# Holding back the loads of a fused adapter kernel until the first gathered rows have landed, and reordering block 0's sums

## The chip, the cores and the metric

The kernel runs on one core of a Trainium2 chip. A time is the device time of one execution in microseconds (us). A core has five engines that run their own instruction streams and meet at semaphores: PE (TensorE, matrix products into PSUM), DVE (VectorE), ACT (ScalarE), POOL (GpSimd) and SP (SyncE, which here issues the plain DMAs). Gathers by index are issued by POOL. Both kinds of DMA are carried out by the same 16 DMA engines, through a queue of SP's (q1 in the profile) and one of POOL's (q0).

## The reference, cut to what matters

x has 64 sequences of 64 tokens with 1024 features, all in fp32. Two adapter layers are added, one after the other:

```python
B_req = B[adapter_ids]                                    # layer 0: one adapter of rank 16 for each sequence
A_req = A[adapter_ids]
x = x + einsum('bnr,bor->bno', einsum('bni,bri->bnr', x, B_req), A_req)

base   = einsum('btd,od->bto', x, W)                      # layer 1: a dense product ...
logits = einsum('btd,ed->bte', x, Wr) + 5.0 * one_hot(language_ids)
topw, topi = top_k(logits, 2)                             # ... and the best 2 of 8 experts of rank 16
gates  = sum(one_hot(topi) * softmax(topw)[..., None], axis=-2)
h      = einsum('btd,erd->bter', x, A)
x = x + base + 2.0 * einsum('bter,bte,eor->bto', h, gates, B)
```

Below, x1 is x after layer 0. The input x is handed over feature-major (xT), W with its input features on the partitions.

## The kernel before, in words

The 4096 tokens are eight blocks of 512 (eight sequences each). Two blocks make a group of tokens (s = 0 to 3), and for each group the 1024 x 1024 product x1 (W + I) is computed by Strassen's scheme with seven products, on two levels; only the first two products of group 0 ("whole" ones, tile pw) stay on one level. The quarter-size weights made on the way in group 0 (tiles s, m) are stored to DRAM (s_kept) and loaded again in the later groups.

What is done for block k:
- `load` brings x in two halves of 512 features, 1 MB each, tiles ("x", k, 0) and ("x", k, 1). SP issues them.
- `gather` brings 128 rows of 4 KB of each adapter table: gb (B) and ga (A), 512 KB each. POOL issues them by the indices idx, which DVE computes from ids0.
- `turn` transposes gb on PE (tile pt, 4 transposes in each of two steps); ACT copies the result out (bt).
- `project` multiplies x by it on PE, 32 matmuls in four column strips (tile pb). A matmul in fp32 is two instructions in the trace, so pb counts x64 for a block. DVE multiplies by a mask (bx).
- `adapt` multiplies bx by ga for each half of the features (tile px, x32 in the trace for a half), and four DVE steps for each half add the result to x in place, a step for each strip of 128 tokens ("gi"). After that the tile holds x1.
- `rows` multiplies x1 by the routers and the experts' A (a1_sb, which holds the loaded a1 and, in its last 8 columns, wr), tile ph, a step of 16 matmul instructions for each strip j of 128 tokens. `gates` is a row of small DVE steps (top 2 and softmax), and `weigh` transposes the gated h (tile pg).
- `early(k)` is turn, project and adapt; `late(k)` is rows, gates and weigh.

The constants: wr_c and ids1 (32 KB each; ids1 is the language id of each sequence, written to all partitions), a1 (512 KB), b1 (512 KB). `languages` computes the router's bias on DVE from ids1, `spread` copies wr into a1_sb on POOL. `add_identity` adds the identity to the four diagonal quarters w_00, w_11, w_22, w_33 of W on DVE, so that the product gives x1 + x1 W.

**The order is made by a planner** (class Plan). Every step is added with its engine and a cost there, the keys that it reads and writes, a due time `at` and the buffers that it takes. `order` runs a list schedule with fixed costs: it picks the engine that can start a step first, and there, among the steps that can start within 0.2 us of that, the one with the smallest due time. A transfer moves 350 KB per us (`KB`), lands 2.2 us later (`LAND`), a gather lands 4.0 + 2.2 us after its issue (`GATHER`). The steps are then issued in the order of their planned starts, and each engine keeps that program order on the chip: a step whose operands are late holds all that stands behind it on its engine. The semaphores themselves come from the tiles that an instruction really touches, not from the planner's keys; a key that names no common tile orders the plan alone.

Buffers: a buffer of a tag is free for the next tile when the last step that reads or writes a key of the old tile is done. Among them are 4 for "l" (PSUM; pt, pb, px, ph and pg take them), 2 for gb, 2 for ga, one each for bt and bx, 7 for "q" (halves of x and their sums).

Due times of the steps around the change, in planner's units: x of block 0 -58, gb of block 0 -59, wr_c and ids1 -53, a1 -45, the w quarters -43 to -36, x of block 1 -42, its gathers -43 and -42, b1 -29; turn -40 for block 0 and -12 for block 1; project -38 and -10; adapt -37 and -36 for block 0, -9 and -8 for block 1; the sums of block 0 -39 and -38; rows of block 0 -14 to -11; add_identity -30; the first product 0.

In the diff: `Plan.add` and `Plan.order` are the planner, `consts` (L308 on) plans the constants, `load` L353, `gather` L367, `project` L400, `adapt` L428, `load_w` L597, `add_identity` L606, and the calls that set due times stand at L988 to L996. The profile puts nearly all instructions on one line (L29, a helper that issues them), so groups are told apart by their tiles.

Of the kernel before, what the change touches and what calls it, by code (L numbers as in the profile page):

```python
# [14 lines left out]
P = 128  # L15
# [18 lines left out]
class Plan:  # L34
# [22 lines left out]
    def add(self, eng, fn, reads=(), writes=(), at=0.0, take=(), kb=0, sb=False):  # L57

        self.steps.append(
            dict(n=len(self.steps), eng=eng, fn=fn, reads=list(reads), writes=list(writes),  # L60
                 at=at, take=list(take), kb=kb, sb=sb)
        )

    def order(self):
        steps = self.steps
        wrote, read, users, tag_of, turns = {}, {}, {}, {}, {}
        for st in steps:
# [16 lines left out]
            st["dep"] = dep  # L84
        held = [[] for _ in steps]
# [6 lines left out]
        for st in steps:  # L92
            for d in st["dep"]:
                after[d].append(st["n"])
        needs = [len(st["dep"]) for st in steps]
        ready = {st["n"] for st in steps if not st["dep"]}
# [9 lines left out]
        def start(n, e):  # L106
            st = steps[n]
            t = clock.get(e, 0.0)
            if st["kb"] and e == "SP":
                t = max(t, moved - self.AHEAD)  # L110
            for d in st["dep"]:
# [66 lines left out]
def kernel(  # L178
# [129 lines left out]
    def consts():  # L308
# [4 lines left out]
        )  # L313
        plan.add({"SP": 0.4}, lambda e: sp.dma_start(a1_sb[:, :, :P], a1), [], [("a1",)], -45, kb=512)
        plan.add({"SP": 0.4}, lambda e: sp.dma_start(b1_sb, b1), [], [("b1",)], -29, kb=512)
# [23 lines left out]
        plan.add({"DVE": 1.0}, languages, [("ids1",)], [("bias",)], -45)  # L339
# [13 lines left out]
    def load(k, i, at):  # L353
        t = ("x", k, i)

        def fn(e):
            made[t] = new("q", [P, HC, TB], f"x_{k}_{i}")
# [7 lines left out]
        plan.add({"SP": 0.5}, fn, [], part(t), at, [("q", t)], kb=1024)  # L365

    def gather(k, tag, table, at):  # L367
# [9 lines left out]
        plan.add({"POOL": 1.1}, fn, [], [((tag, k),)], at, [(tag, (tag, k))], kb=512)  # L377
# [22 lines left out]
    def project(k, at):  # L400
# [3 lines left out]
        def fn(e):  # L404
            made[pb] = new("l", [P, GT], f"pb_{k}")
            made[bx] = new("bx", [P, GT], f"bx_{k}")
            for c in range(NC):
# [11 lines left out]
        def out(e):  # L419
            dve.tensor_tensor(made[bx], made[pb], mask, ALU.mult)  # L420

        plan.add(
            {"PE": 2.2}, fn, [(("bt", k), 1), (("bt", k), 2)] + whole(k), [(pb,), (bx,)], at,
            [("l", pb), ("bx", bx)],
        )
        plan.add({"DVE": 0.3}, out, [(pb,)], [(bx,)], at - 8)

    def adapt(k, h, at):  # L428
# [33 lines left out]
        for gi in range(NG):  # L462
            xs = part(x, gs=[gi])
            plan.add({"DVE": 0.7}, out(gi), [(px[gi],)] + xs, xs, at - 2)
# [132 lines left out]
    def load_w(i, j, at):  # L597
# [6 lines left out]
        plan.add({"SP": 0.4}, fn, [], [(t,)], at, [("s", t)], kb=256)  # L604

    def add_identity(i, at):  # L606
# [8 lines left out]
        plan.add({"DVE": 0.5}, fn, [(t,), (("bx", 0),)], [(t,)], at, sb=True)  # L615
# [372 lines left out]
    consts()  # L988
    for k, at in ((0, -58), (1, -42)):
        for i in range(2):  # L990
            load(k, i, at)
        gather(k, "gb", b0, at - 1)
# [80 lines left out]
```

## Time and profile before

| | |
|---|---|
| runs of the kernel | 528.85, 531.17, 528.12, 528.79 us; median 528.82 |
| the profiled execution | 528.58 us, its span 526.8 us |
| granted PE clock | 0.999 over the span |
| PE busy | 506.6 us (96%) in 3400 matmul instructions |
| DVE busy | 289.9 us (55%) |
| POOL busy | 183.0 us (35%) |
| ACT busy | 41.2 us (8%) |
| DMA | 99.19 MB, mean 188 GB/s over the span; q1 (SP) 90.26 MB, q0 (POOL) 8.39 MB |

The span runs from the first to the last instruction; the time of an execution also has what lies around it. "Busy" of PE counts pipelined matmuls whose ends are modelled, so 96% is not 96% of its peak. The chain that ended last is PE for 94% of the span, DMA for 3%.

The instructions of the opening that the change is about (start and length in us, from the timeline; PE counts are instructions):

| start | length | what |
|---|---|---|
| 1.19 | 0.97 | SP issues x of block 0, both halves |
| 2.21, 2.75, 3.53 | 0.51, 0.74, 0.65 | SP issues wr_c, ids1, a1 |
| 2.88, 4.30 | 1.11, 0.94 | POOL issues gb and ga of block 0 |
| 4.23 | 10.48 | SP issues the first 4 quarters of w |
| 5.54, 6.79 | 0.94, 0.94 | POOL issues gb and ga of block 1 |
| 10.56 | 1.94 | PE pt x8, after 10.56 idle that the landing of gb ended |
| 12.42 | 2.62 | PE pb x64 of block 0 |
| 14.75 | 2.23 | SP issues x of block 1, both halves |
| 14.98 | 0.66 | PE pt x4 of block 1 (the other 4 at 24.77) |
| 15.46 | 1.14 | DVE lang and bias, after 12.58 idle that ids1 ended |
| 16.52 | 0.28 | DVE bx of block 0 |
| 17.03 | 17.62 | SP issues the other 12 quarters of w |
| 18.60 | 0.49 | DVE adds the identity to w_00, after 1.79 idle that w ended |
| 19.01 | 4.87 | DVE sums of block 0, x8 |
| 25.65 | 0.94 | POOL issues gb of block 3, after pt of block 1 |
| 37.93, 39.41 | 1.00, 0.50 | DVE adds the identity to w_22 and w_33; 4.52 and 0.48 idle before them, until w landed |

### The profile page before, as it was taken

The numbers are of one execution on the slowest core, as the hardware profiler recorded it, in microseconds if no ns is written. First come the engines' busy times: TensorE is split into PE (matmuls) and PEld (weight loads), VectorE is DVE, ScalarE is ACT, GpSimd is POOL, SyncE is SP. The second block draws the span as 40 slices with busy tenths as digits, with TensorE's granted clock in tenths as the row PEclk, the third lists the DMA queues.
The fourth block names the chain that finished last, engine by engine and source line by source line (L and its number), as shares of the span: only waits on it lengthen the run. The fifth ranks groups of instructions, "written<-read, shape, count | busy, mean of one in ns | idle before, by whom it ended". The sixth has DMA issues, their size and how long they took to land.

```text
span 526.8 us, 8463 instructions
## 1 busy us (share of the span) xinstructions
PE 506.6 (96%) x3400; PEld 433.2 (82%) x3400; DVE 289.9 (55%) x554; ACT 41.2 (8%) x81; POOL 183.0 (35%) x149
## 2 busy tenths in 40 slices
PE   1799999999999999999999999999999999999995
PEld 1755768798888988898888998889888898888884
DVE  0639999948964174616674355345567417432632
ACT  1111010002000100011000100000200010001000
POOL 3131955762343234222333313312422323433200
PEclk9999999999999999999999999999999999999999
DMA  8999735768666239736556526744545633610222
GB/s 284 362 364 401 277 136 188 272 225 310 215 197 212 82 111 326 255 110 185 176 191 201 189 82 209 268 161 120 162 163 197 205 95 102 218 41 1 80 81 80
DMA packets 53687, 99.19 MB, mean 188 GB/s; under 512 B 4880, under 2 KB 10000, under 8 KB 53648
## 3 DMA queue, kind: packets, MB, share of 16 engines
q1 hardware_dynamic: 51344, 90.26, 50.3%
q0 software_dynamic: 2304, 8.39, 4.3%
q8 instruction: 27, 0.44, 0.3%
q14 instruction: 12, 0.10, 0.0%
HBM read 69.01 MB, written 29.62 MB: 187 GB/s over the span
## 4 chain that ended last, share of the span: by engine, by line
PE 94%; DMA 3%; DVE 1%; issue 1%; SPq 0%; ACT 0%; DVEq 0%
PE pa L29 37%; PE pb L29 35%; PE ph L29 11%; PE pw L29 6%; PE px L29 3%; DMA ids_sb<-in_ids 2%; PE pt L29 1%; DMA out_T<-o 1%; PE pg L29 1%; DVE o L29 1%; SPq L29 0%; DVE bias L29 0%; ACT o L29 0%; DVE lang L29 0%; DVE bx L29 0%
## 5 line engine op out<-in xcount | busy, mean ns | idle before, releaser
L29 PE MATMUL pa<-ti,s 128*128 128x256 f32 x416 | 99.0, 381 | 0.7 <-ACT o L29 0.7
L29 PE MATMUL pb<-ti,s 128*128 128x256 f32 x376 | 93.4, 380 | 0.0
L29 PEld LDWEIGHTS pa<-ti,s 128*128 128x128 f32 x416 | 77.6, 190 | 12.3 <-ACT o L29 1.1
L29 PEld LDWEIGHTS pb<-ti,s 128*128 128x128 f32 x376 | 70.7, 190 | 9.5
L29 POOL TENSOR_TENSOR ti<-x,ti 128x512 f32<-128x512 f32 x28 | 37.2, 1328 | 85.3 <-PE pb L29 84.2
L29 PEld LDWEIGHTS ph<-a_sb,x 128*128 128x128 f32 x512 | 62.7, 190 | 3.8 <-issue 2.7
L29 PE MATMUL ph<-a_sb,x 128*128 128x136 f32 x512 | 63.3, 279 | 2.1 <-issue 2.1
L29 POOL TENSOR_TENSOR ti<-t,ti 128x512 f32<-128x512 f32 x24 | 33.5, 1396 | 87.3 <-PE pb L29 64.8
L29 POOL TENSOR_TENSOR ti<-x 128x512 f32<-128x512 f32 x26 | 34.2, 1314 | 53.2 <-PE pb L29 31.6
L29 DVE TENSOR_TENSOR o<-pb,o 128x512 f32<-128x512 f32 x45 | 31.1, 690 | 34.1 <-PE pb L29 20.6
L29 PE MATMUL pa<-x,s 128*128 128x256 f32 x208 | 49.8, 379 | 0.0
L29 DVE TENSOR_TENSOR x<-px,x 128x512 f32<-128x512 f32 x64 | 39.8, 683 | 10.4 <-PE px L29 6.1
L29 POOL TENSOR_TENSOR ti<-t 128x512 f32<-128x512 f32 x22 | 29.4, 1339 | 44.1 <-PE pb L29 34.4
L29 PEld LDWEIGHTS pa<-x,s 128*128 128x128 f32 x208 | 38.7, 190 | 4.8
L29 PE MATMUL pa<-t,s 128*128 128x256 f32 x168 | 41.2, 381 | 0.8 <-DVE o L29 0.8
L29 PEld LDWEIGHTS pa<-t,s 128*128 128x128 f32 x168 | 31.4, 190 | 5.7 <-DVE o L29 1.2
L29 DVE TENSOR_TENSOR o<-pa,u 128x512 f32<-128x512 f32 x28 | 19.3, 691 | 26.8 <-PE pa L29 26.2
L29 PE MATMUL pw<-x,w 128*128 128x512 f32 x64 | 28.7, 595 | 0.0
L29 DVE TENSOR_TENSOR u<-pb,u 128x512 f32<-128x512 f32 x21 | 14.5, 689 | 25.5 <-ACT u L29 20.7
L29 DVE TENSOR_TENSOR o<-pa,v 128x512 f32<-128x512 f32 x16 | 11.0, 690 | 27.5 <-PE pa L29 24.6
L29 PE MATMUL pb<-hg,b_sb 128*128 128x256 f32 x88 | 26.2, 379 | 0.0
L29 PE MATMUL pb<-x,s 128*128 128x256 f32 x96 | 23.9, 381 | 0.0
(112 smaller groups left out, 577.3 us busy)
## 6 DMA issues: line engine op xcount, KB each, us to landing
s<-s_kept SPq DMA_DIRECT2D x147, 256.0 KB, 2.7
x<-in_xT SPq DMA_DIRECT2D x16, 1024.0 KB, 5.7
out_T<-o SPq DMA_DIRECT2D x32, 512.0 KB, 3.2
s_kept<-s SPq DMA_DIRECT2D x28, 256.0 KB, 4.2
s_kept<-w SPq DMA_DIRECT2D x18, 256.0 KB, 4.8
w<-in_w SPq DMA_DIRECT2D x16, 256.0 KB, 10.1
s_kept<-m SPq DMA_DIRECT2D x3, 256.0 KB, 5.1
a_sb<-in_a SPq DMA_DIRECT2D x1, 512.0 KB, 14.3
```

What stands on the lines that cost most here:

```text
L29: return self._tc.keep_in_program_order(f(*args, **kwargs))
```

## The change

It has these parts:
- The planner learns `behind`: a step that is planned to start after another has started, with no wait on the chip.
- The second x half of block 0 is made by a POOL memset of one column that stands behind the gather of gb of block 0; SP's load of that half waits for the memset. The gather of ga of block 0 stands behind the memset too.
- a1 waits for a POOL copy of one column of the landed gb of block 0 into a1_sb. b1, the w quarters, x of block 1 and every gather of a later block stand behind a1 (`behind`).
- The order of the loads in the program: x half 0, gb, x half 1, ga of block 0, then wr_c, ids1, a1, b1.
- `project` is two steps, one for each half of the features, each needing only its half of x.
- The sums of block 0 get due times that go strip by strip. `languages` and `add_identity` read x of block 0 (the planner's keys): the one is planned after its loads, the other after its sums. `add_identity` no longer reads ("bx", 0).

```diff
--- before.py
+++ after.py
@@ -54,11 +54,12 @@
         self.slots, self.shared = slots, shared
         self.steps = []
 
-    def add(self, eng, fn, reads=(), writes=(), at=0.0, take=(), kb=0, sb=False):
+    def add(self, eng, fn, reads=(), writes=(), at=0.0, take=(), kb=0, sb=False, behind=()):
+
 
         self.steps.append(
             dict(n=len(self.steps), eng=eng, fn=fn, reads=list(reads), writes=list(writes),
-                 at=at, take=list(take), kb=kb, sb=sb)
+                 at=at, take=list(take), kb=kb, sb=sb, behind=list(behind))
         )
 
     def order(self):
@@ -82,6 +83,7 @@
                 users.setdefault(k[0], set()).add(n)
             dep.discard(n)
             st["dep"] = dep
+            st["begun"] = {d for k in st["behind"] for d in wrote.get(k, ())} - dep
         held = [[] for _ in steps]
         left, last = {}, {}
         for tile_ in tag_of:
@@ -90,10 +92,10 @@
                 held[n].append(tile_)
         after = [[] for _ in steps]
         for st in steps:
-            for d in st["dep"]:
+            for d in st["dep"] | st["begun"]:
                 after[d].append(st["n"])
-        needs = [len(st["dep"]) for st in steps]
-        ready = {st["n"] for st in steps if not st["dep"]}
+        needs = [len(st["dep"] | st["begun"]) for st in steps]
+        ready = {st["n"] for st in steps if not needs[st["n"]]}
         free = {tag: [0.0] * c for tag, c in self.slots.items()}
         turn = {tag: 0 for tag in turns}
         clock, end, where, now = dict(self.SET), {}, {}, {}
@@ -108,6 +110,8 @@
             t = clock.get(e, 0.0)
             if st["kb"] and e == "SP":
                 t = max(t, moved - self.AHEAD)
+            for d in st["begun"]:
+                t = max(t, steps[d]["start"] + 0.1)
             for d in st["dep"]:
                 t = max(t, end[d] + (0.0 if where[d] == e and not steps[d]["kb"] else self.LAG))
             want = {}
@@ -311,8 +315,14 @@
             {"SP": 0.4}, lambda e: sp.dma_start(ids1_sb, ids1[0:1, :].to_broadcast([P, NB])),
             [], [("ids1",)], -53, kb=32,
         )
+
+        def hold(e):
+
+            pool.tensor_copy(a1_sb[:, 0, :1], made["gb", 0][:, :1])
+
+        plan.add({"POOL": 0.2}, hold, [(("gb", 0),)], [("a1",)], -56)
         plan.add({"SP": 0.4}, lambda e: sp.dma_start(a1_sb[:, :, :P], a1), [], [("a1",)], -45, kb=512)
-        plan.add({"SP": 0.4}, lambda e: sp.dma_start(b1_sb, b1), [], [("b1",)], -29, kb=512)
+        plan.add({"SP": 0.4}, lambda e: sp.dma_start(b1_sb, b1), [], [("b1",)], -29, kb=512, behind=[("a1",)])
 
         def spread(e):
             pool.tensor_copy(a1_sb[:, :, P:], wr_c)
@@ -336,7 +346,7 @@
             dve.tensor_scalar(bias, bias, LANG_BIAS, None, ALU.mult)
 
         plan.add({"POOL": 0.3}, spread, [("wr_c",)], [("wr",)], -45)
-        plan.add({"DVE": 1.0}, languages, [("ids1",)], [("bias",)], -45)
+        plan.add({"DVE": 1.0}, languages, [("ids1",)] + whole(0), [("bias",)], -45)
 
 
     made = {}
@@ -353,8 +363,16 @@
     def load(k, i, at):
         t = ("x", k, i)
 
+        held = (k, i) == (0, 1)
+
+        def hold(e):
+
+            made[t] = new("q", [P, HC, TB], f"x_{k}_{i}")
+            pool.memset(made[t][:, 0, :1], 0.0)
+
         def fn(e):
-            made[t] = new("q", [P, HC, TB], f"x_{k}_{i}")
+            if not held:
+                made[t] = new("q", [P, HC, TB], f"x_{k}_{i}")
             sp.dma_start(
                 made[t],
                 xT[i * HC * P : (i + 1) * HC * P, k * TB : (k + 1) * TB].rearrange(
@@ -362,7 +380,12 @@
                 ),
             )
 
-        plan.add({"SP": 0.5}, fn, [], part(t), at, [("q", t)], kb=1024)
+        if held:
+            plan.add({"POOL": 0.1}, hold, [], part(t) + [("gathered",)], at, [("q", t)])
+        plan.add(
+            {"SP": 0.5}, fn, [], part(t), at, [("q", t)] * (not held), kb=1024,
+            behind=[("a1",)] * (k == 1),
+        )
 
     def gather(k, tag, table, at):
         def fn(e):
@@ -374,7 +397,10 @@
                 in_offset=bass.IndirectOffsetOnAxis(ap=idx[:, k : k + 1], axis=0),
             )
 
-        plan.add({"POOL": 1.1}, fn, [], [((tag, k),)], at, [(tag, (tag, k))], kb=512)
+        plan.add(
+            {"POOL": 1.1}, fn, [("gathered",)] * ((tag, k) == ("ga", 0)), [((tag, k),)], at,
+            [(tag, (tag, k))], kb=512, behind=[("a1",)] * (k > 0),
+        )
 
     def turn(k, g, at):
 
@@ -401,10 +427,11 @@
 
         pb, bx = ("pb", k), ("bx", k)
 
-        def fn(e):
-            made[pb] = new("l", [P, GT], f"pb_{k}")
-            made[bx] = new("bx", [P, GT], f"bx_{k}")
-            for c in range(NC):
+        def fn(cs):
+            if cs[0] == 0:
+                made[pb] = new("l", [P, GT], f"pb_{k}")
+                made[bx] = new("bx", [P, GT], f"bx_{k}")
+            for c in cs:
                 for gi in range(NG):
                     strip = slice(gi * CG, (gi + 1) * CG)
                     pe.matmul(
@@ -419,10 +446,13 @@
         def out(e):
             dve.tensor_tensor(made[bx], made[pb], mask, ALU.mult)
 
-        plan.add(
-            {"PE": 2.2}, fn, [(("bt", k), 1), (("bt", k), 2)] + whole(k), [(pb,), (bx,)], at,
-            [("l", pb), ("bx", bx)],
-        )
+
+        for h in range(2):
+            plan.add(
+                {"PE": 1.1}, lambda e, h=h: fn(range(h * HC, (h + 1) * HC)),
+                [(("bt", k), 1), (("bt", k), 2)] + part(("x", k, h)), [(pb,)] + [(bx,)] * (1 - h),
+                at + 0.1 * h, [("l", pb), ("bx", bx)] * (1 - h),
+            )
         plan.add({"DVE": 0.3}, out, [(pb,)], [(bx,)], at - 8)
 
     def adapt(k, h, at):
@@ -461,7 +491,7 @@
         )
         for gi in range(NG):
             xs = part(x, gs=[gi])
-            plan.add({"DVE": 0.7}, out(gi), [(px[gi],)] + xs, xs, at - 2)
+            plan.add({"DVE": 0.7}, out(gi), [(px[gi],)] + xs, xs, at - 2 + 1.5 * gi * (k == 0))
 
     def rows(k, at):
 
@@ -601,7 +631,7 @@
             made[t] = new("s", [P, QC, QO], f"w_{i}{j}")
             sp.dma_start(made[t], w[:, j * QC : (j + 1) * QC, i * QO : (i + 1) * QO])
 
-        plan.add({"SP": 0.4}, fn, [], [(t,)], at, [("s", t)], kb=256)
+        plan.add({"SP": 0.4}, fn, [], [(t,)], at, [("s", t)], kb=256, behind=[("a1",)])
 
     def add_identity(i, at):
 
@@ -612,7 +642,7 @@
                 d = made[t][:, c, c * P : (c + 1) * P]
                 dve.tensor_tensor(d, d, ident, ALU.add)
 
-        plan.add({"DVE": 0.5}, fn, [(t,), (("bx", 0),)], [(t,)], at, sb=True)
+        plan.add({"DVE": 0.5}, fn, [(t,)] + whole(0), [(t,)], at, sb=True)
 
     quarter = {
         (i, j): {(k, l): w_name[2 * i + k, 2 * j + l] for k in range(2) for l in range(2)}
@@ -985,12 +1015,13 @@
         for k in rest:
             step(*k)
 
-    consts()
-    for k, at in ((0, -58), (1, -42)):
-        for i in range(2):
-            load(k, i, at)
+    for k, at in ((0, -60), (1, -42)):
+        load(k, 0, at)
         gather(k, "gb", b0, at - 1)
+        load(k, 1, at)
         gather(k, "ga", a0, at)
+        if k == 0:
+            consts()
     for q0, at in (((0, 0), -43), ((0, 2), -39), ((2, 0), -37), ((2, 2), -36)):
         for i, j in ((0, 0), (1, 0), (1, 1), (0, 1)):
             load_w(q0[0] + i, q0[1] + j, at)
```

## Prediction

> **What bounds the kernel now.** I read the table by stretches first, then the chain that ended last, then the DMA issues of the opening, then single waits.
>
> The table by stretches (length, then busy time and instruction count of PE, PE's weight load, DVE, ACT, POOL; then clock, DMA share, GB/s):
>
> ```profile
> 0.00:10.50 10.50, 0.00 (x0) 0.00 (x0) 1.03 (x7) 1.28 (x1) 4.99 (x14) 1.00 0.78 276
> 10.50:16.80 6.30, 5.08 (x76) 4.25 (x76) 1.26 (x5) 1.76 (x3) 1.21 (x2) 1.00 0.91 314
> 16.80:21.00 4.20, 2.08 (x65) 1.92 (x65) 2.40 (x7) 0.00 (x0) 0.94 (x1) 1.00 1.09 370
> 21.00:29.00 8.00, 8.00 (x69) 8.00 (x70) 5.91 (x11) 0.97 (x2) 0.94 (x1) 1.00 1.04 381
> 29.00:39.40 10.40, 10.40 (x29) 4.38 (x31) 4.36 (x22) 1.77 (x4) 4.97 (x4) 1.00 1.08 362
> 39.40:72.50 33.10, 33.10 (x245) 20.34 (x246) 31.28 (x53) 2.74 (x6) 17.19 (x12) 1.00 0.77 294
> ...
> 130.00:515.00 385.00, 384.95 (x2435) 340.09 (x2435) 194.05 (x371) 26.63 (x53) 118.73 (x90) 1.00 0.48 159
> ```
>
> From 21 us on PE is full: 384.95 of 385 us. Only the opening has idle PE that an early change can win: 10.5 + 1.2 + 2.1 = 13.8 us before 21. And in 39.4 to 72.5 DVE is nearly full too (31.28 of 33.1): PE work pulled forward may only meet DVE there.
>
> The chain that ended last, in order of time (start, length, what):
>
> ```profile
> 2.75 12.68 DMA ids_sb<-in_ids
> ...
> 16.86 2.07 PE px L29 x64
> 18.93 2.06 issue
> 20.99 3.95 PE ph L29 x32
> 24.94 0.44 PE pt L29 x4
> 25.37 3.71 PE ph L29 x32
> 29.08 10.30 PE pw L29 x24
> 39.38 1.89 PE pb L29 x64
> ```
>
> The opening hangs on the language ids, which land at 15.43; then px, DVE's sums, ph, and from 29.08 the products pw. Block 1's projection pb runs at 39.38, behind three products.
>
> The DMA issues of the opening, each from a short stretch around it, us to landing last; the second ga is the gather issued at 65.02, when the queues were quiet:
>
> ```profile
> gb<-in_b,idx POOLq DMA_INDIRECT x1, 7.5
> ...
> x<-in_xT SPq DMA_DIRECT2D x1, 1024.0 KB, 12.4
> ...
> x<-in_xT SPq DMA_DIRECT2D x1, 1024.0 KB, 13.7
> ...
> ga<-in_a,idx POOLq DMA_INDIRECT x1, 4.2
> ```
>
> So gb of block 0 (issued 2.88) lands at 10.4, block 1's first half (issued 14.75) at 27.1 and its second half (16.2) at **29.9**. DMA moves 360 to 410 GB/s from 4 us to 45 with one dip, 234 in 12 to 14.5.
>
> **The change, step by step.** Times are those of the profiled execution (528.58 us, span 526.80, so 1.78 around the span; the median of the runs is 528.82, 0.24 more).
>
> 1. First gather. gb0 keeps its place (2.88). Bounds from issue to landing: 4.2 quiet, 7.5 loaded. x half 0 still flows (1 MB from about 3 to 6 us by the rates) and half 1 comes behind; nearer the loaded row: 6.9, landing 9.8 against 10.4. Gain 0.6 (0 to 3.3).
>
> 2. x half 1 of block 0 goes behind a memset that POOL issues after the gather (which ended at 3.99; POOL's next instruction began 0.3 later): SP issues it at 4.5 instead of 1.66, behind wr_c and ids1. Block 0 is 2 x 1.05 + 2 x 0.52 = 3.15 MB; 0.28 had moved by 4 us, the rest at 0.4 MB/us ends at 11.2. The small loads now run in front of it; they are what ran in the dip (2.5 us at 234 instead of 400: 0.42 MB, 1 us). With about 0.6 to land: 12.8, between 11.4 (as before: 1.66 + 9.8) and 14.
>
> 3. pb's second half is half of 1.95 to 2.62, so about 1.1: it ends at 13.9. Languages (1.14 on DVE) stand ahead of bx, but ids1 now lands behind one x half instead of two and a gap of 13 us; with bx 0.28, **px starts at 14.25** instead of 16.86. The memset, the copy that holds a1 and its semaphore cost POOL 0.1 to 0.3 each while it has nothing else: hidden. SP queues a1, twelve more loads and all of x1 behind that copy; a1 then starts near 10.2 instead of 3.53 and needs until about 14 to 15; ph wants it at 17. Hidden, with 2 us of cover.
>
> 4. Sums. The first identity add waited for w (DMA, 1.79 idle) and held the sums from about 18 to 19.01. It goes behind them: 1.0 gained. By strips, ph could start three sums (0.61 each) after px's first half: 14.25 + 1.1 + 1.8 = 17.2.
>
> 5. But block 1's gathers are now behind the copy. gb1 is issued near 10.2; loaded, 7.8 (gb of 13.59): it lands at 18.0. By the planner's figures (landing 6.2 after issue) block 1's two transposes pt fit between px and ph, and PE's order is fixed by them. So ph waits: 18.0 + 0.66 + 0.60 = 19.3. Four strips at 1.86 (7.44): **ph ends at 26.8** instead of 29.08. So far 2.3 won.
>
> 6. What comes next on PE. add_identity read ("bx", 0) before, so the planner's only bx buffer stayed taken until the last identity add; that, not data, put pb of block 1 at 39.3. Now it reads x of block 0 and the buffer is free after px. Worked with the planner's own constants: a1 starts at 11.7, then w x4, gb1, ga1, x1 half 0 (lands 24.5), gb2, half 1 (lands 28.9); ph ends at 29.1. Both halves of pb (due -10) are then ready at their turn and go **ahead of the first pw** (due 0). On the chip PE reaches that point at 26.8 and must wait for x1's second half.
>
> 7. When does that half land? Ahead of it on SP's queue stand the same bytes as before. On POOL's queue there is one gather more: gb3 is issued when pt frees its buffer, at 19.3 instead of 25.65, so 0.52 MB / 0.39 = 1.3 us move ahead of it. The dip at 12 to 14.5 goes (1.1 less) and the loss of step 2 comes (1.0 more). 29.9 + 1.3 - 1.1 + 1.0 = **31.1**. Bounds: 28.7 (no extra gather, no loss), 33 (a further 2 us with an empty queue while a1's copy waits). Then half of pb, 0.95: the products start at 32.05. Before, the same work (ph, then pb's 1.95) was worth 29.08 + 1.89 = 30.97. Net **+1.1**.
>
> 8. Behind that: the same instructions, PE full. Block 1's sums (8 x 0.61) now fall into DVE's gap before 37.9, where it waited 4.52 us for w; so DVE is about 5 us freer in 39.4 to 72.5. b1 stays last on SP (issued 34.92, landed 6.4 later; its readers start at 46.4, so 5 us of cover). The only bubble the change could remove is 0.68 us at 105. I count nothing for it. Cost if wrong: pg of block 1 began 0.15 us after DVE gave up h (71.59 + 0.69, PE at 72.43), so without the relief each us that w lands later is paid.
>
> Sum: -0.6, -2.0 (px), -1.0, given back in step 5 and by the wait of step 6; 528.82 + 1.1 = **529.9**.
>
> The Trainium skill, page "DMA: Bandwidth & Descriptors", section "Queues, rings and completion order", says that each DMA engine goes round between the queues packet by packet; by that, holding SP's loads back gives a gather little, since it would not have stood behind them. Its section "Anatomy of one DMA — SWDGE (gpsimd) path" gives 2.0 us plus bytes over 436 GB/s, for 512 KB an estimate of 3.2 us; the trace has 7.5 and 4.2. With the page's figure gb0 would land at 6.1 and the transposes start 3.7 us sooner; step 7 and so the sum would stay where they are.
>
> **Rivals.**
> Faster: pb of block 1 stays behind products, or x1 lands by 28. Then step 5's 2.3 is kept, 526.5, and up to 3.9 if gb1 lands near 16 (5.8 after issue): 524.9. For it: DVE is freed. Against it: due -10 against 0, and x1's halves landed at 27.1 and 29.9 with 0.5 MB less beside them.
> Slower: block 1's x is starved. Where both queues are busy POOL's moves more (0.29 MB against 0.10 in 19 to 20 us); with gb1 to gb3 and ga1, ga2 all ahead of it, and an empty queue for 2 us at the start, the second half lands at 34: 34 + 0.95 - 30.97 = +4.0, **532.8**. It passes 0.5% when the half lands after 32.6. For it: five gathers now start within 10 us. Against: the bytes are the same.
> No effect: transfers set everything and x1 lands at 29.9 as before: 528.8.
>
> **How the numbers follow.** Forecast 0.55 (its own range 527.5 to 532), slower rival 0.22, faster 0.17, no effect 0.06. A measurement tells 0.5%, 2.6 us, from no change: 526.2 and 531.5 are the borders. Of the faster case three quarters lie below 526.2, 0.13, and 0.01 of the forecast; of the slower case 0.19 lies above 531.5, and 0.08 of the forecast; same is the rest, 0.59. Low 526.3 and high 532.9 leave about 0.1 on each side.
>
> **What would show it.** Right: PE's order pt, pb, px, pt, ph x64, then pb x64 ahead of the first pw, with an idle PE of 2 to 6 us ended by x in that pb; x half 1 of block 1 landing at 30 to 32; px at 13.5 to 15; gb1's wait ahead of ph. Wrong: pw directly behind ph (then 525 to 526); ph waiting for a1; DVE held by ids1; a wait in 40 to 130 on DVE's products or on w.

## The result, and the profile after

The changed kernel takes 529.51 us (median of 52 executions, 528.75 to 532.61) where the kernel before takes 528.94 us beside it (78 executions, 527.79 to 531.34). The ratio is 1.0019, with a 95% interval of 1.0010 to 1.0027: a loss of 0.5 to 1.4 us, which is real and small. The forecast was 529.9 and the border of "no change" 0.5%. The profiled execution took 529.45 us with a span of 527.7, against 528.58 and 526.8.

The 52 executions lie in two groups with nothing between 529.52 and 530.15: 27 around 529.02 and 25 around 531.03. Those of the kernel before do so too, less clearly: 40 around 528.38 and 38 around 529.91. The profile of after is from the lower group; one from the upper group is shown with the last experiment, and explains it. The median of 529.51 is the upper edge of the lower group; with one execution less there it would lie in the gap.

First the table by stretches of after (length, then busy time and instruction count of PE, PE's weight load, DVE, ACT and POOL; then clock, DMA share, GB/s):

```profile
0.00:10.50 10.50, 0.72 (x4) 0.75 (x5) 2.10 (x11) 1.28 (x1) 4.13 (x16) 1.00 0.71 243
10.50:16.80 6.30, 5.89 (x106) 4.77 (x108) 0.29 (x1) 1.17 (x2) 2.38 (x3) 1.00 1.06 366
16.80:21.00 4.20, 3.95 (x60) 3.51 (x54) 4.10 (x7) 1.08 (x2) 1.87 (x2) 1.00 1.05 379
21.00:29.00 8.00, 6.30 (x71) 6.13 (x73) 3.25 (x12) 0.77 (x2) 4.99 (x4) 1.00 1.04 392
29.00:39.40 10.40, 8.78 (x101) 4.79 (x91) 7.49 (x18) 0.80 (x2) 5.04 (x4) 1.00 1.09 356
39.40:72.50 33.10, 33.10 (x160) 19.47 (x159) 28.73 (x57) 3.82 (x8) 11.84 (x9) 1.00 0.59 220
...
130.00:515.00 385.00, 385.00 (x2430) 340.27 (x2423) 192.85 (x370) 26.63 (x53) 118.52 (x90) 1.00 0.49 160
```

Before 21 us PE is busy 3.4 us more than before (0.72 + 5.89 + 3.95 against 5.08 + 2.08). In the next two stretches, where it was full, it now stands still for 1.70 + 1.62 = 3.3 us. The gain of the opening moved into a new hole, and behind 40 us nothing is left to see.

The timeline of PE shows the hole (start and length in us, out<-in and shapes, count; in brackets the idle time before and what ended it):

```profile
9.78 1.94 PE L29 MATMUL pt<-ident,gb 128*128 128x128 f32 x8 [9.78 <-DMA gb<-in_b,idx]
11.65 3.64 PE L29 MATMUL pb<-x,bt 128*32 128x128 f32 x64
15.71 2.07 PE L29 MATMUL px<-bx,ga 32*128 32x128 f32 x64 [0.41 <-DVE bx L29]
17.71 1.19 PE L29 MATMUL pt<-ident,gb 128*128 128x128 f32 x8
19.15 7.65 PE L29 MATMUL ph<-a_sb,x 128*128 128x136 f32 x64 [0.25 <-issue]
28.50 1.08 PE L29 MATMUL pb<-x,bt 128*32 128x128 f32 x32 [1.70 <-DMA x<-in_xT]
31.19 1.08 PE L29 MATMUL pb<-x,bt 128*32 128x128 f32 x32 [1.62 <-DMA x<-in_xT]
32.20 3.70 PE L29 MATMUL pw<-x,w 128*128 128x512 f32 x8
```

Block 1's pb now runs directly behind ph, ahead of the first product pw, and waits for each half of its x. The chain that ended last goes through that load (start, length, what):

```profile
2.88 6.77 DMA gb<-in_b,idx
13.63 17.52 DMA x<-in_xT
```

It lands at 31.15. Added up from PE's records of the whole span: ph of block 0 ends at 29.08 before and 26.80 after; behind it PE is idle for 1.51 and 4.13 us, and works for 491.36 and 491.90. So PE ends at 521.95 and 522.83: 2.28 won, 2.62 given back as waits, 0.54 as work that takes longer, which I did not trace further. I use these three numbers for each experiment below.

### The profile page after: what moved, and what is told of

Same layout as the page of the kernel before. It is cut to its first block, busy times and chain, and to the rows that moved or that the text cites. A ratio compares the mean times of both kernels' runs of the same rounds, so it can differ in the third digit from the quotient of the medians.

```text
span 527.7 us, 8467 instructions
## 1 busy us (share of the span) xinstructions
PE 508.3 (96%) x3400; PEld 433.9 (82%) x3400; DVE 288.8 (55%) x552; ACT 40.8 (8%) x81; POOL 186.2 (35%) x153
## 4 chain that ended last, share of the span: by engine, by line
PE 93%; DMA 5%; SPq 1%; DVE 0%; issue 0%; POOL 0%
PE pa L29 37%; PE pb L29 36%; PE ph L29 10%; PE pw L29 6%; DMA x<-in_xT 3%; PE px L29 3%; DMA gb<-in_b,idx 1%; PE pt L29 1%; PE pg L29 1%; SPq L29 1%; DMA ids_sb<-in_ids 0%; DVE o L29 0%; DVE idx L29 0%; POOL a_sb L29 0%
## 5 line engine op out<-in xcount | busy, mean ns | idle before, releaser
L29 POOL TENSOR_TENSOR ti<-x,ti 128x512 f32<-128x512 f32 x27 | 35.6, 1318 | 79.4 <-PE pb L29 77.5
L29 POOL TENSOR_TENSOR ti<-t,ti 128x512 f32<-128x512 f32 x23 | 32.0, 1393 | 72.4 <-PE pb L29 55.2
L29 POOL TENSOR_TENSOR ti<-t 128x512 f32<-128x512 f32 x24 | 33.4, 1393 | 49.4 <-PE pb L29 34.5
L29 DVE TENSOR_TENSOR o<-pb,o 128x512 f32<-128x512 f32 x45 | 31.1, 690 | 35.7 <-PE pb L29 21.8
L29 DVE TENSOR_TENSOR u<-pb,u 128x512 f32<-128x512 f32 x21 | 14.5, 689 | 25.6 <-ACT u L29 20.7
```

Source lines behind the costliest of these rows:

```text
L29: return self._tc.keep_in_program_order(f(*args, **kwargs))
```

## The experiments

A median stands beside the median of the kernel before on the same chip (528.7, 529.5 and 528.8 in the three groups of runs). The ratio beside it has its 95% interval in brackets. A profile shows one execution: those of the key alone, the order alone and the loads alone are the longest of their runs, that of the gathers held back the second longest.

### The place of block 1's pb

**Later by 11 units of due time**, all else as in after:

```diff
-        project(k, at + 2)
+        project(k, at + 2 + 11 * (k == 1))
```

> The changed kernel with the projection of block 1 (pb) due after the first product, so that PE runs ph, pw, pb, pw. Theory (the wait for x of block 1 in pb, 3.3 us, is what gave the gain of the opening back): pw starts when ph ends, at 26.8 instead of 32.2; pb comes at 30.4, waits under 1 us for the second half of x (landing near 31.2) and the work ph + pb + pw is done at 32.2 to 33 instead of 35.8: 526 to 527, PE full afterwards. Rival (DVE or the landing of w sets 40 to 72, so an earlier PE only waits there): 528.5 to 529.5, with PE idle of 2 to 3 us between 33 and 75 ended by DVE.

527.97 us, ratio 0.9982 (0.9966 to 0.9999). PE in its timeline:

```profile
19.13 7.65 PE L29 MATMUL ph<-a_sb,x 128*128 128x136 f32 x64 [0.25 <-issue]
26.61 3.60 PE L29 MATMUL pw<-x,w 128*128 128x512 f32 x8
30.14 2.16 PE L29 MATMUL pb<-x,bt 128*32 128x128 f32 x64
```

With one product between ph and pb both waits for x are gone at once, and the kernel beats after. So the hole in after comes from pb's place. But only 1.4 of the 3.3 us show in the span (526.3 against 527.7), and the time lies between what the theory (526 to 527) and the rival (528.5 to 529.5) had. The waits of this kernel (engine, waiting group, what it waited for: total, times, longest) name two new ones, for another pb's x at 91 us and for a DVE step at 85 us. A new place for one step shifted the plan behind it too.

```profile
PE pb L29 <- DMA x<-in_xT: 1.0, 1, 1.0
PE pa L29 <- DVE v L29: 0.7, 1, 0.7
```

**The planner's key alone, in the kernel before.** `add_identity` reads x of block 0 in place of ("bx", 0); no load and no other step is touched:

```diff
-        plan.add({"DVE": 0.5}, fn, [(t,), (("bx", 0),)], [(t,)], at, sb=True)
+        plan.add({"DVE": 0.5}, fn, [(t,)] + whole(0), [(t,)], at, sb=True)
```

> The kernel before with one planner key changed: add_identity reads x of block 0 instead of (bx, 0); no load is held back. Theory (that key alone, by freeing the planner's only bx buffer, puts pb of block 1 ahead of the first pw): PE's order is ph, pb, pw; ph ends at 28.6 to 29.1, pb waits for the second half of x (29.9 before) and pw starts at 30.9, worth the same as before (30.97): 528.0 to 529.3. Rival (the buffer has nothing to do with it): the order of before and 528.9. Second rival (the new order costs by itself, because block 1's sums stand behind the identity adds on DVE and px of the second half waits for PSUM): 529.5 to 531 with PE idle of 1 us or more near 42.

528.43 us, ratio 0.9985 (0.9974 to 0.9997). PE:

```profile
28.45 1.08 PE L29 MATMUL pb<-x,bt 128*32 128x128 f32 x32
30.27 1.08 PE L29 MATMUL pb<-x,bt 128*32 128x128 f32 x32 [0.73 <-DMA x<-in_xT]
```

The key alone pulls pb from 39.38 to 28.45. It does two things: it frees the planner's buffer bx earlier, and it puts the identity adds behind the sums (DVE runs them at 23.24), which shortens PE's wait ahead of ph from 2.06 to 1.11 us. That it was the buffer, held by a key that had been put there for order, that kept pb behind three products is shown by the next experiment and by the order alone further down: both have the adds behind the sums and the buffer held, and pb stays behind the products. With the loads in their old order the wait for x is 0.73 us instead of 3.3, and the whole is no loss.

**The other way round: after, with the key put back.** Both keys stand now, so that the adds stay behind the sums:

```diff
-        plan.add({"DVE": 0.5}, fn, [(t,)] + whole(0), [(t,)], at, sb=True)
+        plan.add({"DVE": 0.5}, fn, [(t,), (("bx", 0),)] + whole(0), [(t,)], at, sb=True)
```

> The changed kernel with add_identity reading (bx, 0) again beside x of block 0, so the planner keeps pb of block 1 behind all four first products, as before the change; the loads are held back as changed. Theory (PE keeps the 2.3 us of the opening until DVE, whose work of 40 to 72 cannot start before w_22 and w_33 land near 40 and which has no block 1 sums done by then): pw from 26.8, then PE idle of 1 to 3 us between 40 and 75 ended by DVE or by ACT behind it: 527.5 to 529. Rival (DVE has cover enough): no idle on PE after 26.8 and 526.3 to 527.

526.74 us, ratio 0.9958 (0.9944 to 0.9973). PE:

```profile
26.65 10.46 PE L29 MATMUL pw<-x,w 128*128 128x512 f32 x24
...
40.91 1.95 PE L29 MATMUL pb<-x,bt 128*32 128x128 f32 x64
```

This is after without the hole: up to ph the opening is the same to 0.01 us, three products run at once, and pb finds its x at 40.91. My own theory for this run fell: I had expected DVE to take back a large part of it in 39 to 72 us. In that stretch PE is busy for all 33.10 us and DVE for 30.63 (the row in the form of the tables above):

```profile
39.40:72.50 33.10, 33.10 (x248) 21.14 (x247) 30.63 (x51) 1.56 (x4) 18.48 (x13) 1.00 0.82 306
```

The rival was right: DVE had cover enough.

**The same kernel a second time**, in another group of runs:

> e4 once more, on the chip of e9: 526.5 to 527, 0.4% under the kernel before. If e4 was luck of its chip, 527.5 or more.

526.94 us, ratio 0.9954 (0.9936 to 0.9971). This version beats both kernels, by 0.4 to 0.5% against before; its 14 executions lie between 526.13 and 527.52, in one group.

### What delays block 1's x

**The gathers held back.** In after, POOL reads one column of block 1's second x half before it issues the gather of ga for block 2, so that this gather and all behind it start later:

```diff
+    seen = const.tile([P, 1], F32, name="seen")
...
+            if (tag, k) == ("ga", 2):
+                pool.tensor_copy(seen, made["x", 1, 1][:, 0, :1])
```

> The changed kernel with one POOL copy more, of one column of the second x half of block 1, ahead of the gather of ga of block 2: so that gather and gb of block 3 (1.05 MB) start only when x of block 1 has landed. Order of PE and DVE unchanged. Theory (bytes on the DMA engines set the landing of x, and that sets the start of the products one for one): 1.05 MB / 0.39 = 2.7 us less ahead of it, landing at 28.5 instead of 31.15, pw at 29.5 instead of 32.2, the whole 526.8 (526.3 to 527.6). Rival (queue order or issue on SP sets the landing, not bytes): landing stays at 31 and the time at 529.5. Second rival (landing earlier, but DVE and w set the end): pw at 29.5 and still 529 or more.

528.04 us, ratio 0.9986 (0.9973 to 0.9998). PE:

```profile
29.09 1.08 PE L29 MATMUL pb<-x,bt 128*32 128x128 f32 x32 [0.80 <-DMA x<-in_xT]
30.10 3.70 PE L29 MATMUL pw<-x,w 128*128 128x512 f32 x8
...
39.57 0.66 PE L29 MATMUL pg<-ident,h 128*128 128x128 f32 x4 [1.04 <-DVE x L29]
```

The half lands 2.1 us sooner (29.04 against 31.15) with two gathers less in front of it: they are now issued at 29.81 and 31.09 instead of 18.16 and 19.40. The first gather of this execution landed 0.5 us later than that of after, and with it all loads behind it started later. From issue to landing the half takes 14.9 us instead of 17.5, so the two gathers had delayed it by 2.6 us, 1.3 each. The kernel before has the first of the two at 19.31 already, and the second at 25.65. Half of the 2.1 us is lost again: at 38.5 pg waits 1.04 us for DVE. The theory had 526.3 to 527.6, so the whole is a miss.

### The two halves of the change

**The order alone.** The kernel before, with pb in two halves, the sums strip by strip and ahead of the identity adds, and ("bx", 0) still read; no load is held or moved:

```diff
+        for h in range(2):
+            plan.add({"PE": 1.1}, lambda e, h=h: fn(range(h * HC, (h + 1) * HC)),
...
-            plan.add({"DVE": 0.7}, out(gi), [(px[gi],)] + xs, xs, at - 2)
+            plan.add({"DVE": 0.7}, out(gi), [(px[gi],)] + xs, xs, at - 2 + 1.5 * gi * (k == 0))
...
-        plan.add({"DVE": 0.5}, fn, [(t,), (("bx", 0),)], [(t,)], at, sb=True)
+        plan.add({"DVE": 0.5}, fn, [(t,), (("bx", 0),)] + whole(0), [(t,)], at, sb=True)
```

> The kernel before with the order part alone: pb in two halves, block 0's sums strip by strip, the identity adds behind them (and still holding bx, so pb of block 1 stays behind products); no load is held back. Theory (the loads part gives most of the 2.3 us at the end of ph: it takes ids1 out of the way of bx and lets px start early; the order part gives the 0.5 to 1 us of the identity add): bx still waits for ids1 near 15.4 to 16.5, px at 16.9, ph ends at 28.0 to 28.5 against 29.08: 527.7 to 528.4. Rival (the order part gives it all): ph ends at 27 and 526.7.

528.09 us, ratio 0.9982 (0.9968 to 0.9995). PE:

```profile
16.68 2.07 PE L29 MATMUL px<-bx,ga 32*128 32x128 f32 x64 [0.30 <-DVE bx L29]
19.86 3.94 PE L29 MATMUL ph<-a_sb,x 128*128 128x136 f32 x32 [1.11 <-issue]
```

ph ends at 27.95 instead of 29.08. Of the 1.1 us about 1.0 is PE's wait ahead of ph, 1.11 instead of 2.06 us, since DVE no longer waits for w in front of the sums; the key alone shortens it just as far, so the order strip by strip adds nothing that shows there. The rest is px, which starts 0.18 sooner. Then pg waits 0.71 and 0.58 us for DVE.

**The loads alone.** After, with pb whole, the sums and the keys as before:

```diff
...
-            plan.add({"DVE": 0.7}, out(gi), [(px[gi],)] + xs, xs, at - 2 + 1.5 * gi * (k == 0))
+            plan.add({"DVE": 0.7}, out(gi), [(px[gi],)] + xs, xs, at - 2)
...
-        plan.add({"DVE": 0.5}, fn, [(t,)] + whole(0), [(t,)], at, sb=True)
+        plan.add({"DVE": 0.5}, fn, [(t,), (("bx", 0),)], [(t,)], at, sb=True)
```

> The changed kernel with the loads part alone: loads held back as changed, but pb whole, sums half by half behind the identity add of w_00, bx held by the identity adds as before. Theory (w_00 now stands behind a1, which waits for the first gather: it lands near 20, and the sums of block 0 wait behind its identity add): px at 15.7, the first sum at 20 to 21 instead of 16.9, ph from 22 to 23, ending at 30 to 30.5: 529.8 to 531. Rival (the identity add costs only its 0.5 us): ph ends at 27.3 and 527.2.

532.33 us, ratio 1.0061 (1.0039 to 1.0083), worse than either theory had it. DVE, then PE:

```profile
18.54 0.49 DVE L29 TENSOR_TENSOR w<-w,ident 128x128 f32<-128x128 f32 x2 [3.41 <-DMA w<-in_w]
18.95 4.87 DVE L29 TENSOR_TENSOR x<-px,x 128x512 f32<-128x512 f32 x8
```

```profile
19.69 1.57 PE L29 MATMUL pt<-ident,gb 128*128 128x128 f32 x8 [2.44 <-DVE x L29]
21.05 8.98 PE L29 MATMUL ph<-a_sb,x 128*128 128x136 f32 x64
```

The first quarter of w lands at 18.52, as in the kernel before (18.58), though it is issued at 11.01 instead of 4.23; my theory had 20. It stands ahead of the sums on DVE. DVE has bx done 1.7 us sooner and spends that waiting: 3.41 us of idle DVE instead of 1.79, and the sums start at 18.95 instead of 19.01. So the two halves need each other: holding the loads wins nothing as long as something that waits for w stands ahead of the sums. And ph takes 8.98 us where it takes 7.65 in after: behind PE's wait of 2.44 us the granted clock falls to a half.

```profile
21.00:22.00 1.00, 1.00 (x7) 1.00 (x6) 1.00 (x3) 0.62 (x2) 0.47 (x1) 0.50 1.04 379
```

The same comes once more at 82 us, behind a wait of 2.31 us for DVE. All six executions show a granted clock of 0.991 to 0.997 over the whole. More on that below.

### The opening: gather, x half and small loads

Three kernels on top of the good version (both keys kept).

**The x half not held.** The memset and SP's wait for it go; the second half of block 0 is issued at 2.68, behind the small loads:

```diff
-        held = (k, i) == (0, 1)
+        held = False
...
-        load(k, 1, at)
+        load(k, 1, -52 if k == 0 else at)
```

> The kernel with bx held again (526.74), and x half 1 of block 0 sent without waiting for the POOL memset, right behind wr_c and ids1. Theory (holding that half back by 1.4 us costs block 0 that: its first packets came only near 8 and it landed at 13 to 13.5, after the gathers): lands 0.7 to 1.2 sooner, px at 14.6 to 15.1, ph ends 0.5 to 1 sooner: 525.8 to 526.4. Rival (the gather of gb pays for it, since x then runs beside it): gb lands at 10.4, nothing won: 526.7 to 527.2.

528.00 us, ratio 0.9984 (0.9971 to 0.9996). The gather's rows land at 11.24 instead of 9.66, px starts at 16.57 instead of 15.72 and ph ends at 27.65 instead of 26.81. Holding that one half is worth 1.1 to 1.3 us of the whole (526.94 and 526.74 with it). My theory, by which the gather gains little from it, fell; the rival had the right sign and was too small (526.7 to 527.2).

**The small loads behind the x half.** wr_c and ids1 are issued after it (at 4.80 and 5.35 instead of 1.67 and 2.21):

```diff
-        plan.add({"SP": 0.4}, lambda e: sp.dma_start(wr_c, wr), [], [("wr_c",)], -53, kb=8)
+        plan.add({"SP": 0.4}, lambda e: sp.dma_start(wr_c, wr), [], [("wr_c",)], -53, kb=8, behind=whole(0))
...
-            [], [("ids1",)], -53, kb=32,
+            [], [("ids1",)], -53, kb=32, behind=whole(0),
```

> The kernel with bx held again (526.74), and wr_c and ids1 planned behind x half 1 of block 0. Theory (the small loads run ahead of x half 1 with the DMA engines at 0.43 busy in 6 to 7 us; behind it they cost nothing that block 0 waits for): x half 1 lands 0.5 to 1 sooner, px near 15, 526.0 to 526.5. Rival (small loads crawl beside gathers, as before the change in 12 to 14.5, and ids1 again holds bx): ids1 lands after 15, px at 16.5 or later, 527.5 to 528.5.

527.28 us, ratio 0.9971 (0.9953 to 0.9988). PE, then DVE:

```profile
8.19 1.94 PE L29 MATMUL pt<-ident,gb 128*128 128x128 f32 x8 [8.19 <-DMA gb<-in_b,idx]
...
13.17 1.08 PE L29 MATMUL pb<-x,bt 128*32 128x128 f32 x32 [1.60 <-DMA x<-in_xT]
16.23 2.07 PE L29 MATMUL px<-bx,ga 32*128 32x128 f32 x64 [1.98 <-DVE bx L29]
```

```profile
14.58 0.36 DVE L29 TENSOR_SCALAR lang<-ids_sb 64x32 f32<-64x32 int32 x2 [11.45 <-DMA ids_sb<-in_ids]
```

The gather lands 1.6 us sooner (8.05 against 9.66) and pb ends 1.1 us sooner, but the language ids come at 14.56 and `lang` stands ahead of bx on DVE, as in the kernel before. px starts 0.5 later than with the small loads in front.

**And the languages behind the sums.** The step that computes the bias is planned after block 0's sums:

```diff
-        plan.add({"DVE": 1.0}, languages, [("ids1",)] + whole(0), [("bias",)], -45)
+        return lambda: plan.add({"DVE": 1.0}, languages, [("ids1",)] + whole(0), [("bias",)], -31)
...
     early(0, -40)
+    plan_languages()
```

> The kernel of e8 (bx held again, small loads behind x half 1) with the languages behind block 0's sums on DVE. Theory (in e8 bx waited 1.98 us for ids1 alone; gb lands at 8.2 because nothing small stands in front): px at 14.5 to 14.8 instead of 16.2, ph from 18, ending at 25.7 instead of 27.3, so 525.5 to 526.2 against 527.3 of e8, and below e4. Rival (gb1 or a1 land later than 17 and hold ph, or DVE's chain sets pg): ph ends near 27 and 527.

528.52 us, ratio 0.9985 (0.9973 to 0.9996): a miss. DVE:

```profile
16.30 0.29 DVE L29 TENSOR_TENSOR bx<-pb,mask 128x128 f32<-128x128 f32 x1 [13.26 <-remote]
```

The ids no longer stand in front of bx, and bx still starts at 16.30. By PE's records pb had ended at 14.06; PE's semaphore that releases bx came at 16.28, and the trace has no instruction that it belongs to ("remote"). What held those 2.2 us, and whether it is in every execution, stays open. PE waits 2.59 us ahead of px because of it. The profiled execution (527.78) is also the second shortest of its twelve, with a granted clock of 0.998; eight of the twelve show 0.994 to 0.996. So most executions ran a part at the half clock, which this profile can't show.

**The same move in the version with the order alone**, where nothing is held:

> The kernel of e5 (no load held back, order part alone) with the languages behind block 0's sums on DVE. Theory (with ids1 out of the way pb, whose matmuls end near 15.6, sets bx, and that hangs on gb at 10.4 and on the two halves): px at 16.0 to 16.1 instead of 16.7, ph ends 0.5 sooner than 27.95: 527.5 to 528. Rival (holding the loads back brings nothing that this step does not): px at 15.1 or earlier, ph ends at 26.5 to 27 and the time is that of e4, 526.7.

528.17 us, ratio 0.9982 (0.9970 to 0.9994), the same as without the move (528.09). pb there runs from 12.64 to 16.21 and bx follows at 16.28; with `lang` in front it was 16.34. In this execution there was nothing to win, since pb itself ended that late (I had 15.6). Why it did is told below.

### After, once more

> The changed kernel on the chip of e9 and e4: 0.1 to 0.3% over the kernel before, PE waiting 3.3 us for x of block 1 in pb.

530.39 us, ratio 1.0022 (1.0006 to 1.0037). Its profiled execution is one of the upper group (532.80 us, span 531.0). PE:

```profile
19.18 7.65 PE L29 MATMUL ph<-a_sb,x 128*128 128x136 f32 x64 [0.24 <-issue]
29.25 1.08 PE L29 MATMUL pb<-x,bt 128*32 128x128 f32 x32 [2.42 <-DMA x<-in_xT]
31.91 1.94 PE L29 MATMUL pb<-x,bt 128*32 128x128 f32 x32 [1.57 <-DMA x<-in_xT]
33.77 5.38 PE L29 MATMUL pw<-x,w 128*128 128x512 f32 x8
```

and its table by stretches of 1 us, with the clock third from the end:

```profile
29.00:30.00 1.00, 0.75 (x28) 0.78 (x32) 0.85 (x5) 0.00 (x0) 0.00 (x0) 1.00 1.08 353
30.00:31.00 1.00, 0.33 (x13) 0.06 (x4) 0.07 (x1) 0.21 (x1) 0.00 (x0) 0.67 1.10 353
31.00:32.00 1.00, 0.09 (x4) 0.10 (x8) 0.00 (x0) 0.00 (x0) 0.00 (x0) 0.50 1.09 348
...
37.00:38.00 1.00, 1.00 (x3) 0.38 (x2) 1.00 (x1) 0.00 (x0) 1.00 (x1) 0.91 1.11 362
```

Here the waits are 4.0 us instead of 3.3, and as the second one begins PE's granted clock falls to 0.50 and stays there until 37. The second half of pb takes 1.94 us instead of 1.08, the first products 5.38 instead of 3.70. In the three numbers: ph ends at 26.83, idle 4.80, work 494.55. Against the other execution of the same kernel that is 0.67 more of waiting and 2.65 more of work at half speed.

## Why the prediction was right, point by point

The whole was right (529.9 forecast, 529.51 measured) and so was the mechanism: the gain of the opening is given back in front of block 1's pb. The experiments show the cause from both sides: the key alone brings pb forward in the kernel before, and putting it back in after takes the loss away and about 2 us more (1.6 against the lower group of the kernel before). Two of the signs that I named did not come: px between 13.5 and 15, and a wait for gb1 ahead of ph. Step by step:

1. **First gather.** Forecast 9.8, measured 9.65 (2.88 + 6.77).
2. **x half 1 of block 0.** Forecast 12.8, between 11.4 and 14. pb goes from one half to the other at about 13.4 without a gap, so it was there by then; in three versions with the same loads it landed at 13.19 to 13.59. So it came 0.4 to 0.8 late, and just before a slow pb got to it.
3. **px at 14.25: too early by 1.46.** This is one of two mis-sized terms of the opening; the other is in step 5. I gave pb's second half 1.1 us; it took 1.9, and the first half 1.7, which by itself put the second half at 13.4 (0.8 and 0.6 of the 1.46). In after PE runs all of pb at half pace: each four of its records take 0.21 us from beginning to end, where the records of the kernel before go over from 0.21 to 0.11 at 13.8. I had read 2.62 us for pb off one execution, as if it were a property of the step. A faster pace alone would not have given 14.25: with the pace changing at 12.58 (bx held again, second time) px starts at 15.12, and in the second trace of after (change at 13.28) at 15.74, behind a pause of 0.44 us in pb that the trace doesn't explain.
4. **Sums directly behind px.** Right: they start at 16.90, 1.25 us behind bx, and the identity adds run after them at 21.69.
5. **gb of block 1 at 18.0, ph waits for it.** Off: it landed at 16.2 (10.03 + 6.14) and pt ran at 17.71 without a wait. Steps 3 and 5 are wrong in opposite ways (px 1.46 later, gb1 1.8 sooner), so ph ends at 26.80 where 26.8 was forecast. That agreement is luck.
6. **pb ahead of the first pw.** Right, with 3.3 us of waiting in two pieces.
7. **x lands at 31.1, products at 32.05, net +1.1.** Measured 31.15, 32.20, and +0.9 in the two spans, +0.6 in the medians. One gather more in front of x, 1.3 us, was the reason given; holding back two shortened the transfer of x by 2.6 us, which bears it out. The other two nearly cancel, as I had it: in 12 to 14.5 us DMA moves 346 GB/s where it moved 234, and in 4 to 8 us 308 where it moved 406; at 0.4 MB/us these are estimates of 0.7 us won (1.1 forecast) and 1.0 lost (1.0 forecast).
8. **DVE freer in 39.4 to 72.5, worth nothing.** DVE's busy time there went from 31.28 to 28.73, half of the 5 us forecast, and not as I had it: block 1's sums run at 39.10 to 42.4 and from 45.63 on, not in the gap before 37.9, which the small steps of `gates` fill now. The bubble at 105 went (25.00 of 25 us busy from 105 to 130). The price that I named if that relief were missing was not there: with bx held again DVE is busy for 30.63 and PE does not wait once in the stretch.

**What the sum did not have** is the second cost of a wait. I priced 3 us of idle PE as 3 us; in the execution above they cost 2.65 us more, at a halved clock, and 25 of 52 executions lie 2 us above the others. The forecast still held because without that cost the net loss was smaller than I had it (+0.6 between the lower groups, 529.02 and 528.38), and with it the median of all came to lie 0.4 below the forecast. That the median is so near is luck too: it is the top of the lower group, and twelve further executions have 530.39.

The rivals: the faster one (pb behind products) did not come about, but its price was right: with pb kept behind three products the kernel takes 526.74 and 526.94, and 526.5 was forecast for that order. The slower one needed x after 32.6; it landed at 31.15. The longest executions of after (532.61, 532.80) reach that rival's time, but the traced one by the half clock, with x there by 31.91.

| kernel | ph ends | idle behind it | work behind it | PE ends | ratio |
|---|---|---|---|---|---|
| before | 29.08 | 1.51 | 491.36 | 521.95 | 1 |
| after | 26.80 | 4.13 | 491.90 | 522.83 | 1.0019 |
| after, pb later | 26.78 | 2.55 | 492.08 | 521.41 | 0.9982 |
| after, gathers held back | 27.27 | 2.92 | 492.38 | 522.57 | 0.9986 |
| key alone | 28.53 | 2.21 | 491.52 | 522.25 | 0.9985 |
| order alone | 27.95 | 2.26 | 491.79 | 522.00 | 0.9982 |
| loads alone | 30.03 | 3.72 | 492.73 | 526.48 | 1.0061 |
| after, bx held again | 26.81 | 1.67 | 491.70 | 520.18 | 0.9958 |

The last line is what the change is worth with that key kept: 2.27 us at ph's end, of which 1.77 reach the end of PE.

## What to carry to other kernels

A key that was written down for the sake of order can also hold a buffer, and the buffer can be what keeps a step back: before such a key is replaced, list the steps that take the buffer, and ask for each whether its operands will be there at its new place. Work that is moved forward in one in-order queue waits at its new place for its own transfer, and everything behind it waits too; a due time later by one product was enough here. And a wait on TensorE is to be priced with what may follow at a reduced clock, not by its own length alone.

## What the runs showed of the hardware that I had not expected

**PE's pace has two values, and it changes on a grid of 3.41 us.** In the opening of all kernels pb's records start at 0.21 us for each four, later at 0.11. The granted clock in the tables by stretches reads 1.00 all through, since the list of clock changes in each trace begins with the change to full and the tables count the time before it as full: it stands at 13.85 in the kernel before, 15.19 in after, 10.99 with the small loads behind and 16.01 in the order alone with the languages last, where pb's pace changes at the same times or pb ends before. Counted from PE's first matmul that is 2.80 to 5.67 us in the fourteen traces.

All changes in the lists lie a whole multiple of 3.41 us apart (one stretch of 3.41 us at the half clock twice in the loads alone, two in a row in the second trace of after); the grid begins at another point in each execution. Laid over PE's records, with PE's busy time in single stretches of the grid:

| trace | stretch | PE busy | clock after it |
|---|---|---|---|
| after | 8.36 to 11.77 | 1.99 | stays half |
| after | 11.77 to 15.19 | 3.41 | goes to full |
| before | 10.44 to 13.85 | 3.29 | goes to full |
| after, bx held again | 8.63 to 12.05 | 2.25 | stays half |
| small loads behind | 7.57 to 10.99 | 2.80 | goes to full |
| after | 25.43 to 28.84 | 1.72 | stays full |
| after | 28.84 to 32.25 | 1.80 | stays full |
| small loads behind | 14.40 to 17.81 | 1.58 | stays full |
| after, second trace | 26.93 to 30.35 | 1.08 | falls to half |
| after, second trace | 30.35 to 33.76 | 1.85 | stays half |
| loads alone | 17.07 to 20.48 | 0.97 | falls to half |
| loads alone | 78.51 to 81.92 | 1.10 | falls to half |

No stretch of the fourteen traces goes against this order: the clock falls at the end of stretches with 1.10 us of work or less, never with 1.58 or more; it rises at the end of those with 2.80 or more, never with 2.25 or less. What lies between was not met, and PE's busy time has modelled ends. So pb took 3.64 us in after because PE's first matmul fell into the middle of a stretch, and 2.62 in the kernel before because it fell on the beginning of one; the grid lies differently in each execution, whatever the loads do. And a wait of 2.3 us costs more if it falls into one stretch than if it is split over two: PE's two waits in after were split. One stretch at the half clock costs up to half of 3.41 us, an estimate of 1.7.

The Trainium skill, page "TensorE: Matmul & The Clock Gate", section "Part 1: The HAM clock gate (the "warmup" mystery)", has this: PE runs at half clock until it has been busy through a window of about 3.4 us, the window runs freely and doesn't start with the kernel, and an idle window brings the half clock back. The two paces (0.21 against 0.11), the 0.50 and the grid of 3.41 us agree. Two things differ, and the measurements decide: the page gives a spread of 0.5 us for the moment of the change, here it lies between 2.80 and 5.67 us after the first matmul; and where the page has an idle window, here a window with 2.3 to 2.44 us of idle PE was enough, and one with up to 1.83 was not.

The two groups of times go with the clock. The executions of the lower group of after show a granted clock of 0.997 to 1.000 over the whole, those of the upper group 0.991 to 0.997. Of the kernel before, 50 executions of the three groups of runs lie below 529.2 with 0.998 to 1.000, and 39 from 529.5 up, 38 of them with 0.995 or 0.996. So its upper group too ran a part at the half clock; which of its waits brings that is not shown (its PE waits 2.06 us ahead of ph), since no execution of that group was traced. The versions with 1.1 us there (key alone, order alone, order with the languages last) have no execution above 528.9.

**A gather's landing depends on what SP has queued.** Block 0's first gather, issued at 2.9 to 3.1 in each kernel, took 4.9 and 6.0 us with only x half 0 in front (two traces), 6.1 to 7.2 with the small loads too (after and those with its opening, seven traces), 7.5 to 7.7 with everything queued (before and those with its opening, four) and 8.3 with x half 1 close behind the small loads (one). So executions of one arrangement differ by up to 1.1 us, and the four still don't overlap. The prediction quoted the skill's page "DMA: Bandwidth & Descriptors", section "Queues, rings and completion order", on engines that go round between the queues packet by packet, and drew from it that holding back another queue's loads gives a gather little. That conclusion fell: between the first and the last of the four lie 2.3 to 3.4 us, and the 1.6 us between the x half held and not held were worth 1.1 to 1.3 us in the median. The page's rule itself was not tested here.
